# Four transformer layers on one core: closing steps moved between stages, and half 1 of three feed-forward blocks run two chunks behind half 0

## The chip, the core and the metric

The kernel runs on one core of a Trainium2 chip. A core has five engines with instruction streams of their own: TensorE (PE in the profile, its weight loads PEld), VectorE (DVE), ScalarE (ACT), GpSimd (POOL) and SyncE (SP), which issues most of the DMAs. The metric is the device time of one execution in microseconds.

## The reference

Four layers follow each other over 1024 tokens of 256 features, in float32. Each is an attention, a residual add and a LayerNorm without weights, and then a feed-forward block with the same ending. The eight stages differ; cut to what matters here:

```python
def _layernorm(x): return (x - mean(x)) / sqrt(var(x) + 1e-5)
x = _layernorm(x + L0_attn(x))   # windowed differential attention, 16 heads of 128, 4 key heads
x = _layernorm(x + L0_ffn(x))    # 8 experts, the two best per token
x = _layernorm(x + L1_attn(x))   # causal, 16 heads of 128
x = _layernorm(x + L1_ffn(x))    # ternary weights, SiLU gate, RMS norm of the hidden 1024
x = _layernorm(x + L2_attn(x))   # causal, 16 heads of 16
x = _layernorm(x + L2_ffn(x))    # 4-bit weights, tanh GELU gate, hidden 2048
x = _layernorm(x + L3_attn(x))   # causal, 16 heads of 128, normed queries and keys
x = _layernorm(x + L3_ffn(x))    # 64 experts of 64, the eight best, and a shared one

def L3_ffn(h):
    probs = softmax(h @ router_w.T)
    top = top_8(probs); comb = zeros; comb[top] = probs[top] / sum(probs[top])
    out = sum over e of comb[:, e] * (silu(h @ Wg[e].T) * (h @ Wu[e].T)) @ Wd[e].T
    return out + sigmoid(h @ shared_gate.T) * shared(h)

def L0_ffn(h):
    top2 = top_k(h @ Wr, 2); p = softmax(top2.values)
    return sum over the two of p * ((silu(h @ Wg[e]) * (h @ Wu[e])) @ Wd[e])
```

## The kernel before, in words

The tokens are eight tiles of 128 rows, `x[:, t, :]`, kept in on-chip memory; `xT` holds them turned, so that TensorE can contract over the features. Tiles 0 to 3 are half 0, tiles 4 to 7 half 1; two neighbouring tiles are a pair. The stages are the functions `attn0, ffn0, attn1, ffn1, attn2, ffn2, attn3, ffn3`, called in turn by `four_layers` (L2008), each with memory pools of its own. The eight banks of the matmul memory are shared out anew for each stage: wide tiles of two banks each, the rest single banks. All weights go through ten buffers of the pool "w".

Between the stages a LayerNorm is due. `norm_half` (L191) does four tiles: statistics (`add_stats`, L202 and L203), a root by a ScalarE Sqrt (`rsqrt`, L220, and a reciprocal, L221) or by a GpSimd power (`power`, L213 and L214), and the scaling on VectorE (`norm_tile`, L206). `transpose_two` (L163) turns one pair: four transposes (L171) and a copy (L178). By default `four_layers` turns all four pairs at the start of a stage, and it calls `layernorm` after attention two and attention four.

Inside `k.in_order()` the order of the instructions on PE, ACT, DVE and POOL is the program's own. Outside of it, as in the three feed-forward blocks here, the framework's scheduler sets the order by its own estimate, the earlier in the program the sooner, and may put later instructions where it finds an engine free. A tile's memory is reused when its last reader is done.

*Attention one* (`attn0`) runs 32 units (four groups of heads by eight tiles) in a hand-written pipeline: in iteration i the scores and exponentials of unit i (L659, L667), the mix of unit i-1 (L675 to L695), the values and output projection of unit i-3 (L704 to L722, added to x at L233). In the last group its `close` (L558) ends a pair in four steps, one in each iteration: statistics, root, norm with a DMA of the rows to DRAM (L570) and the turning, router product (L159) with the two best experts (L579 to L582).

*Mixture one* (`ffn0`) makes from these indices a table of slots (to L868), gathers token rows (L226), and runs 23 blocks of 128 rows through the experts' weights (L897, L916), which must be in place as one tile.

*Attention two* (`attn1`) first gathers each token's two results (16 indirect DMAs, L226). Its `close` (L1078) adds the results of a pair (L1082), norms it by `rsqrt` and turns it. After each `close` up to six pieces of the first group's queries are projected (`project_next`: L152, and a copy on ACT, L997); the 16 pieces need only the first pair.

*The three feed-forward blocks* `ffn1` (L1192), `ffn2` and `ffn3` (by `ffn`, L288) go over chunks of 128 hidden units (8, 16 and 33 chunks); for each chunk over both halves of the tokens: gate and up products into two banks (L152, in `ffn1` L1208), the hidden values on ACT and DVE, and the down product (L303, L1234) added up in `acc`, two wide tiles with both halves side by side. `add_ffn` (L310) then copies `acc` (L317), turns it back (L321), adds it to x (L233, L327) and calls `norm_half` for each half.

*Attention four* (`attn3`) runs four groups of heads by eight tiles by four heads. `Pipe` (L385) takes one unit (tile, head) at a time: scores (L281), mask, maximum, exponential (L241, L246, L251), reciprocal and scaling on POOL (L258, L259), turned by L268 and copied (L272). Three units after a tile's last head its values (L1869, L1876) and its output projection (L733, added at L233) follow, a step in each unit. *Mixture four* (`ffn3`) starts with the router for all eight tiles (L159 with `wr`, then the shared expert's gate with `ws`), softmax, the eight best (L1931, L1932), the scaling, two splits into three bfloat16 parts (`split3`) and their turning (`transpose_comb`, L340 and L344) into two tiles `combT`; each chunk spreads its rows of `combT` over the hidden units by a product (L947).

Of the kernel before, what the change touches and what calls it, by code (L numbers as in the profile page):

```python
# [42 lines left out]
class Kit:  # L43
# [244 lines left out]
    def ffn(self, chunks, count, hidden, beside=iter(())):  # L288

        nc = self.nc
        acc = [self.wide() for _ in range(NC)]
        for i, (size, gate, up, down, more) in enumerate(chunks):
            for half in range(2):
                g, u = self.bank()[:size], self.bank()[:size]
                self.project(g, gate, half * HALF, HALF)
                self.project(u, up, half * HALF, HALF)
                h = hidden(g, u, half, more)  # L300
                next(beside, None)
                for m in range(NC):
                    nc.tensor.matmul(  # L303
                        acc[m][:, half * HALF : (half + 1) * HALF],
                        lhsT=down[:, m * P : (m + 1) * P], rhs=h,
                        start=i == 0, stop=i == count - 1,
                    )
        return acc

    def add_ffn(self, acc, scale=None):  # L310

        nc = self.nc
        yT = [self.tile("p4", [P, T]) for _ in range(NC)]
        for half in range(2):
            cols = slice(half * HALF, (half + 1) * HALF)
            for m in range(NC):
                (nc.scalar.copy if m else nc.vector.tensor_copy)(yT[m][:, cols], acc[m][:, cols])  # L317
        for t in range(NT):
            ps = self.bank()[:, :D]
            for m in range(NC):  # L320
                nc.tensor.transpose(  # L321
                    ps[:, m * P : (m + 1) * P], yT[m][:, t * P : (t + 1) * P], self.ident
                )
            if scale is None:
                self.add_rows(t, ps)
            else:
                nc.vector.scalar_tensor_tensor(  # L327
                    self.x[:, t, :], ps, scale[:, t : t + 1], self.x[:, t, :],
                    ALU.mult, ALU.add,
                )  # L330
            if t % 4 == 3:
                self.norm_half(t // 4)

    def transpose_comb(self, parts, n):

        combT = self.tile("w", [3 * n, T], BF16)
        for half in range(2):
            ps = self.bank()[: 3 * n]
            for i in range(4):
                self.nc.tensor.transpose(  # L340
                    ps[:, i * P : (i + 1) * P],
                    parts[:, half * 4 + i].rearrange("p s e -> p (s e)"), self.ident,
                )
            self.nc.vector.tensor_copy(combT[:, half * HALF : (half + 1) * HALF], ps)  # L344
        return combT
# [23 lines left out]
class Pipe:  # L369
# [37 lines left out]

    def finish(self):
        while self.first or self.second or self.queued or self.rest:
# [34 lines left out]
def attn0(k, a):  # L444
# [106 lines left out]

    wr = k.tile("const", [P, NC, 8], tag="wr")
    nc.sync.dma_start(out=wr, in_=a["L0_ffn_Wr"].rearrange("(c p) e -> p c e", p=P))
    logits, k.top = (k.tile("const", [P, NT, 8], tag=n) for n in ("logits", "top"))
    k.which = k.tile("const", [P, NT, 8], U32, tag="which")
    k.rows = k.tile("dram", [T, D], tag="moe_rows")

    def close(t, last=False):  # L558


        stats = k.tile("st", [P, 4, 2], tag="stats", bufs=2)
        k.add_stats(t, stats)
        yield
        k.add_stats(t + 1, stats)
        at = t % 4
        rstd = (k.rsqrt if last else k.power)(stats[:, at : at + 2, 1], 2, LN_EPS)
        yield
        for i in range(2):
            k.norm_tile(t + i, stats, rstd[:, i : i + 1])
        nc.sync.dma_start(  # L570
            out=k.rows[t * P : (t + 2) * P, :].rearrange("(t p) d -> p t d", p=P),
            in_=k.x[:, t : t + 2, :],
        )
        k.transpose_two(t)
        yield
        ps = k.bank()[:, :16].rearrange("p (t e) -> p t e", t=2)
        for i in range(2):
            k.project_rows(ps[:, i, :], lambda c: wr[:, c, :], (t + i) * P)
        nc.vector.tensor_copy(logits[:, t : t + 2, :], ps)  # L579
        for i in (t, t + 1):  # L580
            nc.vector.max(k.top[:, i, :], logits[:, i, :])
            nc.vector.max_index(k.which[:, i, :], k.top[:, i, :], logits[:, i, :])  # L582

    runs = [(g, half) for g in range(4) for half in range(2)]
    closing = {}
    with k.in_order():
# [4 lines left out]
        for i in range(len(units) + 3):  # L591
# [27 lines left out]
            for _ in ending:  # L619
                pass  # L620
            for steps in closing.values():
                next(steps, None)
            if i >= 3 and units[i - 3][0] == 3:
                t = units[i - 3][1]
                if t % 2 == 0:
                    closing[t] = close(t, t == NT - 2)
                    next(closing[t])
        for steps in closing.values():
            for _ in steps:
                pass  # L630
# [1466 lines left out]
```

## Time and profile before

| | us |
|---|---|
| median of 3 runs | 2358.47 (2358.36 to 2358.62) |
| the profiled execution, its own time | 2366.98 |
| its span, first to last instruction | 2365.3 |
| attention one, to its last add to x (L233) | 0 to 299.4 |
| mixture one, to its last expert product | to 402.5 |
| attention two, to its last output projection | to 982.1 |
| ternary block, to its last down product | to 1036.9 |
| attention three, to its last add to x | to 1272.7 |
| second block, to its last down product | to 1450.3 |
| attention four, to its last output projection | to 1964.5 |
| mixture four, to its last down product | to 2349.7 |

The mean granted TensorE clock is 0.970 of full speed. All times below are of the profiled execution, counted from its first instruction. In a timeline each line is start, length, engine, line of the kernel, operation, what it writes and reads with shapes, the count, and in brackets the idle time before it with what ended it. In the chain of waits each piece is start, length, engine, tile and line.

### The profile page before, as it was taken

The page shows a single profiled execution, that of the slowest core. Times are in us where ns is not written, and L with a number is a line of the kernel's source. Part 1 is how long each engine was busy: PE and PEld are TensorE (multiplying, and loading weights), DVE is VectorE, ACT ScalarE, POOL GpSimd, SP SyncE. Part 2 cuts the span into 40 slices and gives each one's busy share as a digit, 9 for nine tenths or more (in the row PEclk, how much of TensorE's full clock was granted, in tenths as well). Part 3 has the DMA queues.
Part 4 walks back from the last instruction along what each step waited for, and adds up shares of the span by engine and source line. Part 5 has one row for each costly group of instructions (what it writes and reads, how often), then busy time and mean ns, then how long its engine had stood idle before and what let it go on. Part 6 is the DMA issues. An engine that isn't in the chain of part 4 may idle for free.

```text
span 2365.3 us, 25450 instructions
## 1 busy us (share of the span) xinstructions
PE 2175.3 (92%) x8595; PEld 1228.6 (52%) x8595; DVE 1219.0 (52%) x2726; ACT 904.5 (38%) x2345; POOL 493.5 (21%) x633
## 2 busy tenths in 40 slices
PE   7999767899999999998898998899999997999997
PEld 4666544566656655664444443455555564444443
DVE  5677556465665646555763445544544554222223
ACT  3666523334343434344453222454544451111111
POOL 4333221222232323321110000332222220000000
PEclk9999879899999999989999999999999998999999
DMA  5100163011102101013100010000000000111000
GB/s 167 43 18 20 41 196 109 25 41 36 50 22 63 54 27 41 19 54 119 53 2 10 27 54 27 2 1 18 1 18 10 10 1 18 36 45 45 20 2 18
DMA packets 59250, 92.24 MB, mean 39 GB/s; under 512 B 8976, under 2 KB 33616, under 8 KB 59120
## 3 DMA queue, kind: packets, MB, share of 16 engines
q1 hardware_dynamic: 54208, 78.15, 10.5%
q0 software_dynamic: 4912, 12.46, 1.9%
q8 instruction: 69, 1.13, 0.2%
q14 instruction: 61, 0.50, 0.1%
HBM read 69.76 MB, written 17.17 MB: 37 GB/s over the span
## 4 chain that ended last, share of the span: by engine, by line
PE 78%; DVE 10%; ACT 6%; issue 2%; DMA 2%; POOL 1%; SPq 1%; another core or an unknown queue 0%; ACTq 0%; DVEq 0%; POOLq 0%
PE bank L152 23%; PE wide L281 10%; PE wide L303 7%; PE bank L1063 5%; PE bank L268 5%; PE bank L1869 5%; PE bank L159 4%; PE bank L733 3%; ACT e L667 2%; PE bank L1048 2%; PE bank L1460 1%; PE bank L722 1%; PE bank L1208 1%; PE bank L897 1%; ACT pt L1485 1%
## 5 line engine op out<-in xcount | busy, mean ns | idle before, releaser
L152 PE MATMUL bank<-xT,w 128*128 128x512 f32 (+2 forms) x1520 | 663.3, 566 | 3.3 <-DVE xT L178 2.5
L152 PEld LDWEIGHTS bank<-xT,w 128*128 128x128 f32 (+1 forms) x1520 | 288.5, 195 | 282.2 <-issue 259.3
L259 POOL TENSOR_SCALAR p<-p,st 128x128 f32<-128x128 f32 (+7 forms) x256 | 191.8, 749 | 678.5 <-DVE st L258 535.7
L281 PE MATMUL wide<-k,q 128*128 128x512 f32 (+3 forms) x768 | 290.3, 487 | 3.6 <-ACT p L251 2.7
L272 ACT COPY pt<-bank 128x512 f32<-128x512 f32 (+3 forms) x384 | 171.0, 480 | 307.5 <-PE bank L268 304.3
L281 PEld LDWEIGHTS wide<-k,q 128*128 128x128 f32 x768 | 142.5, 190 | 140.5 <-issue 125.3
L246 DVE TENSOR_REDUCE st<-wide 128x1 f32<-128x128 f32 (+7 forms) x256 | 194.1, 758 | 14.4
L303 PE MATMUL wide<-t,w 128*128 128x512 f32 (+1 forms) x392 | 187.5, 600 | 3.9 <-DVE t L1737 2.4
L268 PE MATMUL bank<-ident,p 128*128 128x128 f32 x1152 | 169.2, 274 | 18.7 <-POOL p L259 18.6
L268 PEld LDWEIGHTS bank<-ident,p 128*128 128x128 f32 x1152 | 137.7, 141 | 83.0 <-issue 38.8
L1987 DVE TENSOR_TENSOR t<-t,bank 128x512 f32<-128x512 f32 (+1 forms) x66 | 45.4, 688 | 258.0 <-PE bank L152 249.5
L1986 ACT ACTIVATE t<-bank 128x512 f32<-128x512 f32 (+1 forms) x66 | 39.4, 597 | 324.4 <-PE bank L152 314.8
L1063 PE MATMUL bank<-pt,v 128*128 128x512 f32 (+3 forms) x384 | 139.3, 487 | 0.0
L241 DVE TENSOR_TENSOR wide<-wide,causal 128x128 f32<-128x128 f32 x256 | 74.7, 292 | 121.7 <-PE wide L281 120.7
L1869 PE MATMUL bank<-pt,v 128*128 128x512 f32 x288 | 137.2, 596 | 0.0
L251 ACT ACTIVATE p<-wide,st,factor 128x128 f32<-128x128 f32 (+7 forms) x128 | 106.5, 832 | 71.2 <-DVE st L248 70.5
L303 PEld LDWEIGHTS wide<-t,w 128*128 128x128 f32 (+1 forms) x392 | 68.0, 189 | 109.4 <-issue 47.4
L251 ACT ACTIVATE p<-wide,st 128x128 f32<-128x128 f32 (+7 forms) x128 | 95.1, 743 | 65.1 <-DVE st L246 64.4
L159 PE MATMUL bank<-w,xT 128*128 128x512 f32 (+2 forms) x288 | 116.0, 540 | 0.5 <-ACT v L541 0.5
L667 ACT ACTIVATE e<-wide,st 128x128 f32<-128x128 f32 x256 | 90.1, 378 | 51.3 <-DVE st L659 36.6
L1485 ACT ACTIVATE pt<-wide 128x1024 f32<-128x1024 f32 (+3 forms) x96 | 75.7, 811 | 70.0 <-PE wide L1479 68.1
L233 DVE TENSOR_TENSOR x<-bank,x 128x256 f32<-128x256 f32 x120 | 49.8, 421 | 88.8 <-PE bank L1048 34.5
(310 smaller groups left out, 3059.5 us busy)
## 6 DMA issues: line engine op xcount, KB each, us to landing
w<-in_L_ffn_gate_up_dram SPq DMA_DIRECT2D x16, 512.0 KB
w<-in_L_attn_Wq_dram SPq DMA_DIRECT2D x12, 512.0 KB
w<-in_L_attn_Wo_dram SPq DMA_DIRECT2D x12, 512.0 KB
rows<-parts SPq DMA_DIRECT2D x16, 256.0 KB
w<-in_L_ffn_down_dram SPq DMA_DIRECT2D x8, 512.0 KB
w<-in_L_attn_Wk_dram SPq DMA_DIRECT2D x7, 512.0 KB
w<-in_L_attn_Wv_dram SPq DMA_DIRECT2D x6, 512.0 KB
moe_results<-y SPq DMA_DIRECT2D x23, 128.0 KB
```

The source lines that it names most:

```text
L152: self.nc.tensor.matmul(out, lhsT=weight(c), rhs=self.xcols(c, lo, n), start=c == 0, stop=c == NC - 1)
L159: self.nc.tensor.matmul(out, lhsT=self.xcols(c, lo, n), rhs=weight(c), start=c == 0, stop=c == NC - 1)
L246: nc.vector.tensor_reduce(top, scores[:, :n], axis=AX.X, op=ALU.max, negate=True)
L251: nc.scalar.activation(probs[:, :n], scores[:, :n], AF.Exp, bias=top, scale=1.0 if scale is None else scale, accum_out=total,)
L259: self.nc.gpsimd.tensor_scalar(probs[:, :n], probs[:, :n], total, 1.0, ALU.mult, ALU.mult)
L268: self.nc.tensor.transpose(ps[:, i * P : (i + 1) * P], probs[:, (lo + i) * P : (lo + i + 1) * P], self.ident,)
L272: self.nc.scalar.copy(pts[lo // 4][:, :n, slot * P : (slot + 1) * P], ps[:, : n * P].rearrange("p (b q) -> p b q", b=n),)
L281: self.nc.tensor.matmul(s[:, lo : lo + m], lhsT=query, rhs=key(lo, m), start=True, stop=True)
L303: nc.tensor.matmul(acc[m][:, half * HALF : (half + 1) * HALF], lhsT=down[:, m * P : (m + 1) * P], rhs=h, start=i == 0, stop=i == count - 1,)
L667: nc.scalar.activation(e[:, r, f, b, :], sc[:, r, f, b, :], AF.Exp, bias=top[:, at : at + 1], accum_out=total[:, at : at + 1],)
L1063: nc.tensor.matmul(out[:, lo:], lhsT=values[g, b][:, h * P : (h + 1) * P], rhs=pts[b // 4][:, b % 4, lo:], start=b == 0, stop=b == 4 * hal ...
L1869: nc.tensor.matmul(out, lhsT=values[i][:, g * P : (g + 1) * P], rhs=pts[i // 4][:, i % 4, :], start=i == 0, stop=i == b,)
```

## The change

1. `attn0` loses its closing steps. `four_layers` calls `layernorm` after it and turns all pairs at the start of `ffn0`; `ffn0` writes the rows to DRAM in two DMAs of one half each and makes the router product, maxima and indices for all tiles at once.
2. In `attn1` the closing of a pair is split in three functions, and query pieces are put between them: with counts 0, 3, 4 and 5 for the four pairs, all but one between the adding and the root, one between the root and the norm.
3. `ffn` and `ffn1` run half 1 two chunks behind half 0 (`LAG`), and end half 0 (copies, turning, adds, norm) before the last three half-chunks of half 1. `add_ffn` takes one half.
4. `attn3` gets a `close` for a pair in eight steps: power, norm, turning, router product with the shared gate in a 65th column, softmax (the gate by an exponential instead of a sigmoid), eight best, combination, and for each of the two groups of experts a split and a turning. One step follows each unit of the last group. What is left runs in `ffn3` after half 0 of the first chunk (`before`). The `layernorm` after `attn3`, the turning at the start of `ffn3` and its router part go.

The core of the diff:

```diff
-    def ffn(self, chunks, count, hidden, beside=iter(())):
+    LAG = 2
+    def ffn(self, chunks, count, hidden, before=iter(())):
         acc = [self.wide() for _ in range(NC)]
+        held = {}
+        def add_up(i, half):
+            size, gate, up, down, more = held[i] if half == 0 else held.pop(i)
+            g, u = self.bank()[:size], self.bank()[:size]
+            self.project(g, gate, half * HALF, HALF)
+            self.project(u, up, half * HALF, HALF)
+            h = hidden(g, u, half, more)
+            for m in range(NC):
+                nc.tensor.matmul(
+                    acc[m][:, half * HALF : (half + 1) * HALF],
+                    lhsT=down[:, m * P : (m + 1) * P], rhs=h, start=i == 0, stop=i == count - 1,
+                )
+        for i in range(count + self.LAG):
+            if i < count:
+                held[i] = next(chunks)
+                add_up(i, 0)
+            for _ in before:
+                pass
+            if i == count - 1:
+                self.add_ffn(acc, 0)
+            if i >= self.LAG:
+                add_up(i - self.LAG, 1)
+        self.add_ffn(acc, 1)
...
-    def transpose_comb(self, parts, n):
+    def transpose_comb(self, parts, combT, t):
+        n = combT.shape[0]
+        ps = self.bank()[:n, : 2 * P]
+        for i in range(2):
+            self.nc.tensor.transpose(
+                ps[:, i * P : (i + 1) * P], parts[:, i].rearrange("p s e -> p (s e)"), self.ident
+            )
+        self.nc.vector.tensor_copy(combT[:, t * P : (t + 2) * P], ps)
...
@@ attn1
-        for t in range(0, NT, 2):
+        for t, count in ((0, 0), (2, 3), (4, 4), (6, 5)):
+            add_results(t)
+            for i in range(count - 1):
+                project_next()
+            take_root(t)
+            if count:
+                project_next()
             close(t)
-            for _ in range(6 if pieces[0][:2] == (make_queries, 0) else 0):
-                if pieces[0][:2] == (make_queries, 0):
-                    project_next()
...
@@ ffn1 (add_up(i, half) is the loop's former body)
+    def finish(half):
+        ps = k.bank()[:, :4]
+        for i in range(4):
+            at = (4 * half + i) * P
+            nc.tensor.matmul(
+                ps[:, i : i + 1], lhsT=squares[:, at : at + P], rhs=k.ones, start=True, stop=True
+            )
+        norm = k.rsqrt(ps, 4, float(np.finfo(np.float32).eps), 1.0 / 1024)
+        k.add_ffn(acc, half, norm)
+    for i in range(8 + k.LAG):
+        if i < 8:
+            add_up(i, 0)
+        if i == 7:
+            finish(0)
+        if i >= k.LAG:
+            add_up(i - k.LAG, 1)
+    finish(1)
...
@@ attn3
+    wr = k.tile("w", [P, NC, 65])
+    k.combT = [k.tile("w", [99, T], BF16) for _ in range(2)]
+    def close(t):
+        at = t % 4
+        rstd = k.power(stats[t // 4][:, at : at + 2, 1], 2, LN_EPS, tag="root")
+        yield
+        for i in range(2):
+            k.norm_tile(t + i, stats[t // 4], rstd[:, i : i + 1])
+        yield
+        k.transpose_two(t)
+        yield
+        ps = k.bank()[:, :130].rearrange("p (t e) -> p t e", t=2)
+        for i in range(2):
+            k.project_rows(ps[:, i, :], lambda c: wr[:, c, :], (t + i) * P)
...
+        nc.scalar.activation(probs, probs, AF.Exp)
+        nc.scalar.activation(gate, ps[:, :, 64], AF.Exp, scale=-1.0)
+        yield
...
+        for group in range(2):
+            yield
+            parts = k.tile("t2", [P, 2, 3, 33])
+            k.split3([parts[:, :, i, :] for i in range(3)], comb[:, :, group, :], [P, 2, 33])
+            k.transpose_comb(parts, k.combT[group], t)
+    def close_on():
+        if k.closing and next(k.closing[0], k) is k:
+            k.closing.pop(0)
...
+        if g == 3:
+            if b % 4 == 0:
+                stats[b // 4] = k.tile("st", [P, 4, 2], tag="stats", bufs=2)
+            k.add_stats(b, stats[b // 4])
+            if b % 2:
+                k.closing.append(close(b - 1))
...
@@ ffn3
-    k.add_ffn(k.ffn(chunks(), 33, hidden))
+    k.ffn(chunks(), 33, hidden, (step for steps in k.closing for step in steps))
@@ four_layers
-            mine = {ffn0: (), attn1: (), ffn1: (), ffn2: (), attn2: (0, 2)}
+            mine = {attn1: (), ffn1: (), ffn2: (), attn2: (0, 2), ffn3: ()}
-            if stage in (attn1, attn3):
+            if stage in (attn0, attn1):
                 k.layernorm()
```

## The prediction

> **What bounds the kernel now.** I read first the page's engine totals, then the busy time by stretches (one row for each stage boundary that the diff touches), then the timeline at those boundaries, and last the chain of waits in the end of the first attention.
>
> ```profile
> PE 2175.3 (92%) x8595; PEld 1228.6 (52%) x8595; DVE 1219.0 (52%) x2726; ACT 904.5 (38%) x2345; POOL 493.5 (21%) x633
> ```
>
> TensorE is busy 92% of the span, so 190 us are left in which it is not. Where they lie is seen by stretches (start:end, length, then busy us of PE, PEld, DVE, ACT and POOL, the granted clock, DMA share):
>
> ```profile
> 278.00:299.00 21.00, 15.47 (x66) 11.38 (x65) 7.37 (x30) 6.13 (x17) 2.85 (x8) 0.84 0.24 74
> 299.00:322.00 23.00, 5.88 (x48) 4.53 (x47) 12.71 (x58) 3.07 (x4) 4.54 (x5) 0.60 0.94 305
> 417.00:448.00 31.00, 22.54 (x81) 17.52 (x80) 13.98 (x37) 11.05 (x19) 6.99 (x8) 0.79 0.12 37
> 1034.00:1049.00 15.00, 9.89 (x45) 8.09 (x45) 12.02 (x38) 4.06 (x7) 1.27 (x1) 0.61 0.27 88
> 1446.00:1464.00 18.00, 9.79 (x37) 5.72 (x38) 13.70 (x42) 3.58 (x6) 0.00 (x0) 0.81 0.25 84
> 1860.00:1951.00 91.00, 89.35 (x360) 54.28 (x358) 50.09 (x145) 49.05 (x107) 24.20 (x35) 1.00 0.03 7
> 1965.00:1991.00 26.00, 13.06 (x97) 12.57 (x98) 17.85 (x59) 4.96 (x6) 0.00 (x0) 0.71 0.14 41
> 1991.00:2347.00 356.00, 355.21 (x855) 151.11 (x853) 91.07 (x132) 39.40 (x66) 8.52 (x29) 1.00 0.08 25
> 2347.00:2366.00 19.00, 4.66 (x20) 2.32 (x20) 11.01 (x37) 2.95 (x5) 0.00 (x0) 0.71 0.16 56
> ```
>
> The bodies are TensorE-bound (355.21 of 356 us in the last mixture, 89.35 of 91 in the fourth attention's last heads); the boundaries are VectorE chains under which TensorE waits. The widest is between attention four and its mixture:
>
> ```profile
> 1962.50 1.99 PE L733 MATMUL bank<-w,ot 128*128 128x256 f32 x8 [0.79 <-DVE ot L1876]
> ...
> 1972.32 0.69 DVE L1923 TENSOR_REDUCE st<-bank 128x8 f32<-128x512 f32 x1 [2.45 <-PE bank L159]
> ...
> 1990.83 4.76 PE L152 MATMUL bank<-xT,w 128*128 128x512 f32 x8
> ```
>
> From the end of the last output projection (1964.49) to the first gate product (1990.83) are 26.3 us. At the end of the second mixture:
>
> ```profile
> 1448.35 1.98 PE L303 MATMUL wide<-t,w 128*128 128x512 f32 x4 [2.39 <-DVE t L1737]
> 1449.51 1.29 DVE L317 COPY p<-wide 128x512 f32<-128x512 f32 x2 [1.22 <-PE wide L303]
> ...
> 1462.08 1.91 PE L159 MATMUL bank<-w,xT 128*128 128x512 f32 x2
> ```
>
> Both halves of the accumulator are copied only after half 1 is done, and attention four starts 11.8 us after the last down product. In the first attention the pairs' closing steps stand in the chain itself:
>
> ```profile
> 261.79 0.54 DVE x L206
> 262.33 0.04 issue
> 262.37 0.88 PE bank L171 x4
> 263.25 0.02 issue
> 263.28 0.69 DVE xT L178
> ```
>
> **What the Trainium skill says.** "TensorE: Matmul & The Clock Gate", Part 1: the matrix clock falls to half after an idle window of about 3.4 us and comes back after as long a busy one. The trace agrees: the granted clock is 0.60 to 0.84 in these stretches and 1.00 in the bodies, and eight L722 took 3.78 us at 282.30 and 1.99 at 290.21. "ScalarE: Activation LUTs", What ACT_TABLE_LOAD costs: 1283 ns and a drain after it. The load is 1.28 us here; no drain shows (the load at 1948.92 is followed by its Sqrt at 1950.21). "Perfetto Trace Analysis", Tensor Engine Instruction: ScalarE and VectorE run strictly in their order. At 429.56 a Sqrt whose input was ready at 421.48 runs behind six query copies.
>
> **The change, part by part**, all against the profiled span.
>
> *Attention four to the last mixture.* Removed: the 26.3 us. Put in their place, by pairs: of TensorE per pair four L171 (two pairs took 1.09, so 0.57), eight router loads and products (28 took 3.24: 0.93; the gate's own 32, 3.68 us, go into the same 65 columns), four turns of weights (16 L340 took 3.71: 0.93), together 2.43. Three pairs lie in the last heads, which have no slack: 7.3, less the 0.8 and 1.45 us for which TensorE waited at 1962 and 1952, of which I take little: +7. Pair four lies in the mixture: +2.4. Per pair VectorE gets some 35 small operations, about 9.5 us at 0.17 to 0.43; eight units of some 3.4 us have 27 us and VectorE is 55% busy there, so this fits, but is queued ahead of the next unit's mask and maximum: I take +1 in all. POOL gets a power of 0.69 in place of the Sqrt and its table. Each step has a unit of its own, so what waits behind it is the next unit's softmax, then L268. Pair four's chain from the last L733 is 16 to 19 us (add 0.43, statistics 0.65, power 0.95, norm 0.75, turn and copy 1.9, router 1.9, softmax with a table load 2.5, top eight 2.5, two splits 3, turns 2). The half 1 that needs it starts after three half-chunks of 5.37 = 16.1 us, and needs the weights some 1.7 later: a stall of 0 to 4, taken as 2. Bank release 0.5. Sum: -26.3 + 7 + 1 + 2.4 + 2 + 0.5 = **-13.4** (-20 to -5). SP now issues the router's two loads at attention four's start instead of at 1498, and three of the ten weight buffers (router, two turned weights) are taken before the mixture; its first weights were issued from 1635 on, so neither is a bound.
>
> *Ends of three blocks.* Half 0 ends three half-chunks ahead, so its copies, turns, adds and norm lie beside TensorE's bodies. Instructions in the bodies stay; a bank tile more or less isn't asked for. Last block: after its L317 at 2348.91 only four tiles follow. VectorE then has four adds (1.42), four statistics (2.25) from 2350.83: 2354.5; root and reciprocal 0.6; norm 1.4: 2356.5 instead of 2360.33. The output DMA was issued at 2360.36 and moves with it: **-3.9**. Second mixture block: copies end 1450.9, first add frees a bank at 1451.8, turn 0.6 and copy 0.7 of the already normed half, attention four's rows start at 1453.6; before, they started at 1462.08, stopped, and went on at 1464.26, worth 1463.2: -9.6, less 1 for half 0's work on the last chunks: **-8.5** (-10 to -5). Ternary block: 1036.93 to 1048.96 were 12.0. Squares now 1037.35 to 1038.3, root and reciprocal 0.55, first scaled adds 1039.3 to 1040.6, turn, copy, first product 1042.3: -6.6. Against it its ScalarE is busy 1.84 of 2.91 us per half-chunk and gets a root between Silus, two loads of 1.28; VectorE gets 6.5 us in 8.7 where 4.2 are taken: +1.6. **-5** (-7 to -1).
>
> *Second attention's start.* Roots no longer wait behind six copies. Pair 2: statistics 421.48, root 422.9 behind two copies, turn done 424.9 (before 431.75). Pair 4: statistics 428.9, root 430, turn done 431.8 (441.8). Pair 6: 435.9, 436.4, 437.9 (447.6). Then four queries of 0.86 are still due before keys: 441.4 against 447.44: **-6** (-8 to -2). The gathers (the last issued at 425.18) bound it from below.
>
> *First attention undone.* Score exponentials of its last units end 7.15 us apart where nothing is put between and 7.8, 9.6, 7.35, 7.14 after 246.18: without closings the last end is 274.8, not 278.08. Then three turns of 5.1 with the first at 4.9: the last add ends at 290.3, not 299.40. Then in series what was spread: statistics, root, reciprocal 1.2, four norms 1.4, last turn and copy 1.6, routers (32, of which 16 lie under the norm) to 7.2, one copy and eight maximum and index pairs of 0.36, 3.1: 10.3 to the last index, where one pair took 7.5. Then 9.4 to the first gather as now: 310.0 against 316.25. Half 0's norm falls in the drain and may hold a copy there: +1. SP: the rows' two writes stand ahead of the expert weights; these start when the last L710 frees their place, 288 against 296.24, and took 20 us, so they land by 311 even with 2 us of stall, before the first expert product at 316. **-5** (-8 to +3; the upper end if the roots fall between exponentials or the weights wait for the second write).
>
> Sum: -13.4 - 3.9 - 8.5 - 5 - 6 - 5 = -41.8. The profile's own time is 2366.98 (span 2365.3), 8.5 over the median 2358.47; a difference carries over: 2358.5 - 41.8 = 2316.7, 2317.
>
> **Rivals.** One: closings cost in attention four what they cost in attention one, 3.3 us for four units, 0.83 a step; 24 steps are 20 us in place of the 1: 2336. For it: the same in-order queues. Against: here each step has a unit and TensorE, not a chain through ScalarE, is the bound. Chance 0.14. Two: the copies of half 0 still wait for half 1 (L317 did so while VectorE idled from 2341.98), as both lie in one tile: the block ends keep their tails, +17.4: 2334. Against: in the new order the copies stand ahead of half 1's last three. Chance 0.08. Three: the first attention gives back 3 instead of gaining 5, 2325; it shares the forecast's case. Slower: the closing steps' waits stand wholly in the unit chain, at the 2.5 us that turn, copy and statistics took at 261.79 to 264.5; 24 steps are 60 us in place of the 1: 2376. It decides above (41.8 + 1) / 24 = 1.8 us a step. Chance 0.05. No change, if the rivals add up: 0.02. Forecast 0.71.
>
> **Range.** The bounds of the parts added in squares give some 9 either way; the first two rivals reach to 2336. 2302 to 2338. A difference of 0.2% (4.7 us) is what a measurement of this kernel tells from none. Faster 0.93, same 0.02, slower 0.05.
>
> **What would show it.** Right: the first gate product within 3 us of the last L733, and L317 in two groups some 15 us apart; first gather near 310; turns at 424, 431, 437. Wrong: TensorE waiting for VectorE between L281 and L268 in attention four; gaps in the first three half-chunks; expert products waiting for weights.

## The result, and the profile after

The changed kernel takes 2347.44 us (median of 5 runs, 2345.31 to 2349.54) where the kernel before took 2358.62 beside it: a ratio of 0.9955 (0.9944 to 0.9966), a gain of 11.2 us where 41.8 were forecast. The span of its profiled execution is 2347.5 us.

A second profiled execution of the kernel before (first experiment) has a span of 2358.7, so it, not the first one of 2365.3, is the one to subtract from. The stages, measured from TensorE's products:

| stretch | before, first | before, second | after | forecast of the difference |
|---|---|---|---|---|
| start to the first expert product | 322.2 | 321.3 | 321.9 | -5 |
| mixture one's last product to attention two's first score | 47.6 | 41.8 | 37.8 | -6 |
| ternary block, first to last down product | 43.8 | 43.8 | 51.7 | +1.6 |
| from there to attention three's first wide product | 17.9 | 16.3 | 13.2 | -6.6 |
| second block, first to last down product | 163.8 | 163.8 | 165.0 | +1 |
| from there to attention four's first row product | 11.8 | 11.7 | 7.8 | -9.6 |
| attention four, first product of values to last output projection | 455.3 | 455.5 | 467.6 | +8 |
| from there to the last block's last down product | 385.2 | 386.6 | 369.7 | -21.4 |
| from there to the end | 15.5 | 15.7 | 10.7 | -3.9 |

Against the second execution the rows give +0.6, -4.0, +7.9, -3.1, +1.2, -3.9, +12.1, -16.9 and -5.0. They sum to -11.1; the stages that the table leaves out differ by some us either way and cancel.

The engine totals of the page:

```profile
PE 2168.4 (92%) x8563; PEld 1222.0 (52%) x8563; DVE 1228.8 (52%) x2799; ACT 913.7 (39%) x2358; POOL 492.8 (21%) x637
```

TensorE's share has not risen. Busy time of the changed kernel by stretches, with the columns as before:

```profile
294.00:322.00 28.00, 11.20 (x75) 9.85 (x72) 15.01 (x74) 3.07 (x4) 4.86 (x5) 0.56 0.86 276
...
1850.00:1941.00 91.00, 83.27 (x346) 50.83 (x345) 61.29 (x205) 42.64 (x99) 21.42 (x32) 1.00 0.02 7
...
1973.00:2337.00 364.00, 357.30 (x865) 152.50 (x864) 101.11 (x180) 44.08 (x73) 8.44 (x29) 0.99 0.09 27
```

Attention four's last heads were full (89.35 of 91 us) and now leave TensorE idle for 7.7 of 91: the closing steps brought waits and not only work. The last block, 355.21 of 356 before, now has 6.7 us of idle time. The boundary itself went as forecast (timeline of the changed kernel):

```profile
1965.10 1.99 PE L701 MATMUL bank<-w,ot 128*128 128x256 f32 x8 [1.11 <-DVE ot L1944]
1966.93 3.60 PE L152 MATMUL bank<-xT,w 128*128 128x512 f32 x8
...
1972.06 1.08 PE L159 MATMUL bank<-w,xT 128*128 128x65 f32 x8 [0.87 <-DVE xT L178]
...
1978.37 0.76 PE L351 MATMUL bank<-ident,t 128*99 128x128 f32 x4 [3.46 <-DVE t L363]
```

The first gate product follows the last output projection at once. But the turning of pair four's splits (L351) then stands in TensorE's queue for 3.46 us until VectorE has made the splits.

### The profile page after: what moved, and what is told of

The parts are those of the page before. It is cut to its first block, busy times and chain, and to the rows that moved or that the text cites. A ratio compares the mean times of both kernels' runs of the same rounds, so it can differ in the third digit from the quotient of the medians.

```text
span 2347.5 us, 25446 instructions
## 1 busy us (share of the span) xinstructions
PE 2168.4 (92%) x8563; PEld 1222.0 (52%) x8563; DVE 1228.8 (52%) x2799; ACT 913.7 (39%) x2358; POOL 492.8 (21%) x637
## 4 chain that ended last, share of the span: by engine, by line
PE 68%; issue 11%; DVE 10%; ACT 6%; DMA 2%; POOL 1%; SPq 1%; DVEq 0%; ACTq 0%; POOLq 0%
PE bank L152 18%; PE wide L281 9%; PE bank L1047 5%; PE wide L306 5%; PE bank L268 5%; PE bank L1937 4%; PE bank L159 3%; ACT e L635 3%; PE bank L701 3%; PE bank L1032 2%; PE bank L1464 1%; PE bank L881 1%; PE bank L1202 1%; DVE st L627 1%; PE bank L690 1%
## 5 line engine op out<-in xcount | busy, mean ns | idle before, releaser
L281 PE MATMUL wide<-k,q 128*128 128x512 f32 (+3 forms) x768 | 290.6, 487 | 3.7 <-ACT p L251 2.8
L281 PEld LDWEIGHTS wide<-k,q 128*128 128x128 f32 x768 | 142.1, 190 | 136.6 <-issue 121.3
L306 PE MATMUL wide<-t,w 128*128 128x512 f32 (+1 forms) x392 | 188.5, 603 | 4.9 <-DVE t L2026 3.2
L268 PE MATMUL bank<-ident,p 128*128 128x128 f32 x1152 | 169.3, 274 | 21.4 <-POOL p L259 20.0
L268 PEld LDWEIGHTS bank<-ident,p 128*128 128x128 f32 x1152 | 137.7, 141 | 85.6 <-issue 39.0
L306 PEld LDWEIGHTS wide<-t,w 128*128 128x128 f32 (+1 forms) x392 | 68.3, 189 | 109.4 <-issue 48.0
L159 PE MATMUL bank<-w,xT 128*128 128x512 f32 (+3 forms) x320 | 122.8, 521 | 1.7 <-DVE xT L178 0.9
```

Source lines behind the costliest of these rows:

```text
L159: self.nc.tensor.matmul(out, lhsT=self.xcols(c, lo, n), rhs=weight(c), start=c == 0, stop=c == NC - 1)
L268: self.nc.tensor.transpose(ps[:, i * P : (i + 1) * P], probs[:, (lo + i) * P : (lo + i + 1) * P], self.ident,)
L281: self.nc.tensor.matmul(s[:, lo : lo + m], lhsT=query, rhs=key(lo, m), start=True, stop=True)
L306: nc.tensor.matmul(acc[m][:, half * HALF : (half + 1) * HALF], lhsT=down[:, m * P : (m + 1) * P], rhs=h, start=i == 0, stop=i == count - 1,)
```

## The experiments

Unless said otherwise each kernel is the changed kernel with one edit. The kernel before, run beside each, took 2358 us in some sessions and 2365 to 2366 in others (those of *later*, *roots on GpSimd*, *rows first*, *steps apart*, *left out* and attention one's second run), of which some 6 us lie in attention two's start (38 and 44 us from mixture one's last product to the first score, with the same code). So the ratios to the kernel before of the same session are compared, and stages that an edit leaves alone serve as a measure of chance. In the profiles with an untouched ternary block its body took 51.1 to 52.2 us, the last block's (first to last down product) 361.3 to 365.1; smaller differences there say nothing.

**The kernel before, again.** No edit.

> The kernel before, unchanged, for a second profiled execution. The first one took 8.5 us more than the median of the others. Theory: these 8.5 us lie where its TensorE ran at a clock of 0.79, in the query products of attention two (24 L152 in 7.72 us at 418.38), so here attention two's first score product (L281) starts near 443 and not at 450.1, and the span is near 2357. Rival: the 8.5 us are spread over all stages, or lie elsewhere, and L281 starts at 450 again.

Its profiled execution has a span of 2358.7 (ratio 1.0004, 0.9996 to 1.0012). Busy time at attention two's start:

```profile
405.00:444.00 39.00, 22.25 (x87) 16.67 (x88) 19.32 (x52) 13.58 (x22) 15.54 (x16) 0.78 0.20 58
```

L281 starts at 443.37. Of the 6.6 us by which the first span is longer 5.8 lie in that stretch; 2.9 in attention three and smaller differences of both signs make up the rest. So over a third of the 17.8 us that the two first spans show is no gain. The clock is low in this execution too (0.78 in the first row), so my reason, the clock, is not the whole of it.

**Attention one's exchange undone.** `attn0` and `ffn0` as before, twice:

```diff
+            for steps in closing.values():
+                next(steps, None)
...
-    for t in range(NT):
-        k.project_rows(ps[:, t, :], lambda c: wr[:, c, :], t * P)
```

> The changed kernel with attention one's closing steps and mixture one's router as in the kernel before. Theory from the two traces: the exchange is worth nothing, because the 5.4 us by which attention one ends earlier are used up by the router in series, so the first expert product stays within 1 us of 321.9 and the median is 2347 to 2348. Rival, the prediction's step: the change gained 5 there, so this is 2352.

> The changed kernel with attention one and mixture one as before, a second time: are its 4.7 us the exchange or a chance of the clock? If the exchange: the first expert product at 318 to 319.5, where the changed kernel has 321 to 325, and a ratio to before under 0.9945. If chance: 321 to 322, 0.9955 to 0.9965.

Ratios 0.9933 (0.9920 to 0.9946) and 0.9951 (0.9935 to 0.9967); the changed kernel has 0.9955 and, a second time, 0.9966 (0.9952 to 0.9979). The first expert product comes at 318.1 and 319.1, in eleven profiles with the exchange at 321.0 to 325.0. So my first expectation, no effect, was wrong: beside these kernels the exchange costs some 3 us. The second ratio lies between what I had said for an effect and for chance. One reason is seen in the changed kernel's timeline of TensorE:

```profile
297.14 2.89 PE L159 MATMUL bank<-w,xT 128*128 128x8 f32 x14
...
299.88 0.88 PE L171 MATMUL bank<-ident,x 128*128 128x128 f32 x3
300.55 3.85 PE L159 MATMUL bank<-w,xT 128*128 128x8 f32 x18
```

Three of the last pair's four turns (L171 at 299.88) stand behind fourteen router products of other tiles (L159), and the 32 router products take 0.21 us each in a stretch where the clock is 0.56. In the prediction 16 of them lay under the norm; here the first starts at 297.14, when the norm (L206, to 297.24) is just done. What stays open: the same instructions of attention one took 321.3 and 322.2 in the kernel before. Half clock was granted there for 37.5 us between 240 and 330, and for 27.3 in the two kernels here; why, no run shows.

**Attention four's closing steps undone.** `attn3` and the router as before:

```diff
-                    close_on()
...
+    for t in range(NT):
+        k.project_rows(logits[:, t, :], lambda c: wr[:, c, :], t * P)
```

> The changed kernel with attention four without closing steps and the last mixture's router as in the kernel before, in series. Theory from the two traces: the closing steps cost attention four 12.3 us and the mixture some 6 in stalls and added products, against the 26.3 us gap and the 0.6 that go; undoing loses only 3 to 8: 2350 to 2355. Attention four, from its first row product to its last output projection, is 12 us shorter than in the changed kernel. Rival, the prediction's step: 13.4 us, so 2361.

2355.46 us, 0.9985 (0.9976 to 0.9994): 0.0030 more than the changed kernel, about 7 us. Attention four's stretch is 455.3 again, the mixture's 388.9. The steps are worth 7, not 13.4.

**Half 0 ended last.** `add_ffn(acc, 0)` and `finish(0)` after the loop:

```diff
-            if i == count - 1:
-                self.add_ffn(acc, 0)
...
+        self.add_ffn(acc, 0)
         self.add_ffn(acc, 1)
```

> The changed kernel, half 1 still two chunks behind, but half 0's copies, turning, adds and norm come after the last half-chunk of half 1 in all three blocks. Theory: what half 0's early end gains after the last product it costs before it, so the ternary block ends 3 us earlier than in the changed kernel (its last half-chunks lose their 8 us of stall), the second block 3 later, the last 2 later: 2347 to 2351. Rival, the prediction's steps: early ends were worth 17.4 us, so 2365.

0.9951 (0.9940 to 0.9963), the same as with early ends. The ternary block's body is 43.8 (51.7) and what follows 16.0 (13.2): the early end loses 5.2 there. Second block: 163.9 and 11.7 (165.0 and 7.8): it gains 2.8. Last block: 358.8 and 15.0 (363.8 and 10.7): it gains nothing, 0.7 the other way. Three early ends that were forecast at 17.4 us lose 3 in the stages and gain nothing clear of chance in the ratio, and the question is what they cost inside the bodies. The last 17 us before the ternary block's last down product, in the kernel before (second execution) and the changed kernel:

```profile
1015.00:1032.00 17.00, 16.41 (x70) 11.73 (x68) 7.87 (x12) 9.07 (x18) 7.45 (x6) 1.00 0.20 61
```

```profile
1018.00:1035.00 17.00, 13.67 (x52) 9.21 (x52) 10.64 (x26) 11.23 (x16) 3.68 (x4) 0.90 0.20 63
```

TensorE was busy for 16.41 us at full clock, and now is for 13.67 at 0.90. The timeline of the changed kernel's ternary block:

```profile
1016.36 1.53 PE L1227 MATMUL wide<-t,w 128*128 128x512 f32 x4 [0.94 <-ACT t L183]
...
1017.69 0.69 DVE L330 COPY p<-wide 128x512 f32<-128x512 f32 x1 [0.59 <-PE wide L1227]
...
1018.32 1.05 PE L1237 MATMUL bank<-ones,p 128*128 128x1 f32 x8 [0.43 <-POOL p L1224]
...
1020.95 7.37 PE L1202 MATMUL bank<-parts,w 128*128 128x512 f32 x24 [0.37 <-DVE x L340]
...
1026.86 2.37 DVE L206 TENSOR_SCALAR x<-x,st,st 128x256 f32<-128x256 f32 x4
...
1029.15 0.68 DVE L184 TENSOR_TENSOR t<-t,t 128x512 fp32r<-128x512 f32 x1
...
1029.88 0.74 PE L1227 MATMUL wide<-t,w 128*128 128x512 f32 x2 [1.09 <-DVE t L184]
1031.13 1.53 PE L1227 MATMUL wide<-t,w 128*128 128x512 f32 x4 [0.51 <-ACT t L183]
1033.52 1.53 PE L1227 MATMUL wide<-t,w 128*128 128x512 f32 x4 [0.86 <-ACT t L183]
```

Half 0's last products (L1227), the sums of squares (L1237) and the turns (left out here) stand in TensorE's order ahead of half 1's gate products, with waits of 0.94, 0.43 and 0.37 us. Then TensorE does the gate and up products of all three half-chunks that are left in one go (24 L1202). Only down products are left behind them, and these wait 1.09, 0.51 and 0.86 us for half 1's hidden values, with nothing to fill the time. The first of the three waits for L184, which ran behind the scaling of half 0's norm (L206). The next five kernels take suspects away.

**Later.** The end one half-chunk later:

```diff
             if i >= self.LAG:
                 add_up(i - self.LAG, 1)
+            if i == count - 1:
+                self.add_ffn(acc, 0)
```

> The changed kernel, half 0's end (copies, turning, adds, norm) one half-chunk of half 1 later in all three blocks. Theory: in the changed kernel TensorE stands in front of half 0's turns (waits of 0.9, 0.4 and 0.4 us in the ternary block, 0.8 and 1.8 in the others); a half-chunk put ahead covers these. The ternary block, from its first to its last down product, falls from 51.7 to 49 to 50 us, the second block's from 165.0 to 164, the last one's from 363.8 to about 361.5; what follows the last products stays; median near 2342. Rival, ScalarE's roots and table loads hold back the hidden values: no change in the ternary block, 2346.

0.9963 (0.9951 to 0.9975); the ternary block takes 52.3, the second 167.7, the last 362.3. In the ternary block the waits at half 0's end shrink from 1.74 to 1.32 us in all, but at the end of the block TensorE waits 1.35 and 1.96 us for the last hidden values, behind which nothing is left to do. In the second block a wait of 2.39 us for hidden values stands ahead of half 0's turns. My expectation was wrong in two blocks of three; the last one's 1.6 lie within chance.

**Roots on GpSimd.** Half 0's roots by `power`:

```diff
-        norm = k.rsqrt(ps, 4, float(np.finfo(np.float32).eps), 1.0 / 1024)
+        norm = (k.rsqrt if half else k.power)(ps, 4, float(np.finfo(np.float32).eps), 1.0 / 1024)
```

> The changed kernel with half 0's roots (the ternary block's own and the three norms') as a power on GpSimd, so that ScalarE loads no table between half 1's last hidden values. Rival (ScalarE): of the ternary block's 7.9 lost us the 3.1 go for which TensorE waited at L1227 after 1028, so 51.7 becomes 48.5; 2344. Theory (TensorE's order alone): 51 to 52, 2347.

0.9956 (0.9942 to 0.9969), the ternary block 52.4. Its timeline:

```profile
1032.46 2.34 DVE L206 TENSOR_SCALAR x<-x,st,st 128x256 f32<-128x256 f32 x4 [1.13 <-POOL st L214]
...
1034.72 0.68 DVE L184 TENSOR_TENSOR t<-t,t 128x512 fp32r<-128x512 f32 x1
```

ScalarE is free, but the scaling now waits for GpSimd in VectorE's queue, and half 1's low part (L184), on which TensorE waits, stands behind it. The wait changed engines.

**The norm called later, and left out.** The first calls half 0's norm after the loop; the second leaves out the norm of half 0's four tiles after this block; the third in addition takes the block's own root to GpSimd:

```diff
-        self.norm_half(half)
+        if norm:
+            self.norm_half(half)
```

> The changed kernel; in the ternary block half 0's copies, turning and adds stay where they are, its norm comes after the last half-chunk. Theory now: it is the norm, by its statistics and scaling on VectorE (4.3 us) as much as by its root on ScalarE, that holds back half 1's last hidden values, so that moving the root to GpSimd gained nothing; without it the block falls from 51.7 to 48 to 48.5 (2.4 us of moved TensorE work and 1.7 of waits remain) and what follows grows by 1 or 2. Rival, TensorE's wait at half 0's turns, which stays here: 51 to 52.

> The changed kernel with half 0's LayerNorm after the ternary block left out (its copies, turns and adds stay), so that it can't be put back among half 1's hidden values, as the scheduler did with the norm that was called later. If the norm holds them back (ScalarE 1.6 us of table and root between two Silus, VectorE 4.3 us): first to last down product 51.5 falls to 48 to 49.5. If TensorE's order (waits of 1.7 us at half 0's turns and 2.4 us of moved products) and the block's own root are the cause: 50.5 to 52.

> As the one before, and the ternary block's own root for half 0 as a power on GpSimd, so that ScalarE loads no table for half 0. If norm and table loads are what holds the hidden values back: 47 to 48.5, that is 43.8 plus 2.4 us of moved products plus 1.7 of waits. If TensorE's order alone: 51 again.

The first has 0.9962 (0.9948 to 0.9975) and 51.5 us, but tests nothing: the scheduler put the norm back among half 1's hidden values (L206 at 1030.56, where the block's last down products are at 1037.2), as it may outside `in_order`. With the norm left out the block takes 49.9 us (ratio 0.9938, 0.9925 to 0.9951), with the root moved too 50.9 (0.9952, 0.9936 to 0.9969). My theory of the norm had said 48 to 49.5 and 47 to 48.5, its rival 50.5 to 52 and 51: the block gained 1 to 2 us, less than the theory said. What is left is seen in the stretches of the kernel without the norm (TensorE's busy time first, its clock third from the end):

```profile
1022.00:1026.00 4.00, 3.06 (x12) 1.52 (x10) 2.15 (x4) 2.79 (x5) 1.35 (x2) 1.00 0.02 8
1026.00:1030.00 4.00, 3.52 (x16) 3.03 (x16) 1.23 (x4) 2.13 (x3) 1.21 (x1) 0.67 0.00 0
1030.00:1034.00 4.00, 4.00 (x13) 3.31 (x12) 1.39 (x4) 1.33 (x2) 0.00 (x0) 0.50 0.02 4
```

After the waits at half 0's end the granted clock falls to half, and half 1's products run behind it at half speed. So the body must be divided into waits and clock. From its first to its last down product, in us:

| kernel | body | TensorE idle in it | half clock granted in it |
|---|---|---|---|
| before, second execution | 43.8 | 0.5 | 0 |
| changed | 51.7 | 4.4 | 3.41 |
| changed, second profile | 51.2 | 4.0 | 3.41 |
| later | 52.3 | 4.7 | 7.72 |
| roots on GpSimd | 52.4 | 4.3 | 7.54 |
| norm called later | 51.5 | 4.6 | 3.41 |
| norm left out | 49.9 | 2.3 | 6.83 |
| norm left out, root on GpSimd | 50.9 | 3.0 | 6.83 |
| half 0 ended last | 43.8 | 0.9 | 0 |

The idle time is the body less TensorE's busy time. Two of the rows that it is taken from, the changed kernel and the one without the norm:

```profile
983.40:1035.05 51.65, 47.20 (x189) 33.62 (x187) 27.61 (x50) 30.03 (x50) 18.72 (x15) 0.97 0.16 52
```

```profile
992.40:1042.30 49.90, 47.55 (x189) 35.26 (x187) 23.33 (x37) 27.21 (x47) 18.77 (x15) 0.93 0.17 53
```

In the seven profiles whose ternary block is that of the changed kernel the idle time is 3.9 to 4.5 us, and half clock 3.41, in one of them 4.91. So the norm does hold TensorE up: without it 1 to 2 us of the waits go. But half clock was granted for 6.83 us in these two kernels, 3.41 more than in the changed one. As the clock is halved, that is worth at most 1.7 us, an estimate from the granted clock, and about as much as the shorter waits brought. In the changed kernel's second profile the body of 51.2 us divides so, against the kernel before: 3.5 us more idle time, 1.2 for the eight turns, and 2.8 by which the busy time of the same 180 other products is longer (46.04 us, not 43.29). Half clock explains at most 1.7 of these 2.8; for the rest no run shows a cause.

**Rows first.** Attention four turns half 1 just before its rows:

```diff
+    pieces += [(k.transpose_two, t) for t in (4, 6)]
     pieces += [(make_rows, t) for t in range(4, 8)] + [(norm_rows, 1)]
```

> The changed kernel, attention four turns only half 0 at its start and half 1's pairs just before their rows. Theory: the first row product waited at 1453.03 behind half 1's turns in TensorE's queue; now it stands 5.4 us after the last down product and not 7.8, and the first product of values (L1937) is earlier by as much, 51.9 and not 54.3 after it: 2345. Rival, VectorE's norm of half 1 is what the rows wait for, in its queue: the values stay at 54, 2347.

0.9942 (0.9928 to 0.9955). The changed kernel's timeline at this place, and then this one's:

```profile
1451.15 2.08 PE L171 MATMUL bank<-ident,x 128*128 128x128 f32 x8 [2.67 <-DVE x L206]
...
1453.03 14.57 PE L159 MATMUL bank<-w,xT 128*128 128x512 f32 x32
```

```profile
1450.98 1.09 PE L171 MATMUL bank<-ident,x 128*128 128x128 f32 x8 [0.85 <-DVE x L233]
...
1453.54 2.84 PE L159 MATMUL bank<-w,xT 128*128 128x512 f32 x6 [1.47 <-DVE xT L178]
```

In the changed kernel all sixteen turns stand ahead of the first row product, and the last eight wait 2.67 us for half 1's norm. Here the rows start 4.75 us after the last down product (7.8), and attention four ends 518.4 us after it instead of 521.9. The first product of values came at 44.6 and not at the 51.9 that I expected, but attention four takes 6 us longer from there on, so that time is no measure of the gain.

**Steps apart.** Each turning of a split a unit after its split; pair four's steps over two half-chunks:

```diff
-            k.transpose_comb(parts, k.combT[group], t)
+            k.turns.append((parts, k.combT[group], t))
...
-            for _ in before:
+            for _ in zip(range(99 if i else 6), before):
```

> The changed kernel, each turning of a split (L351) a unit after its split, and in the last mixture pair four's first six steps after half 0 of chunk 0, the others after half 0 of chunk 1. Theory: TensorE stood 3.5 us in attention four and 3.5 in the mixture before turns whose split was issued in the same step. Attention four, from its first product of values to its last output projection, falls from 467.6 to 464, the mixture's end after it from 369.7 to 366.5; 2340. Rival, the closing steps' VectorE work delays the units and the wait only moves: 467 and 369, 2347.

0.9927 (0.9913 to 0.9941). Attention four's stretch is 463.7, where ten profiles without the edit show 466.7 to 467.7; the mixture's, 368.3, lies within chance. There TensorE still stands for 1.95 us before a down product (L306 at 1983.41), where it stood for 3.46 before the turn. The waits in attention four, in the changed kernel:

```profile
1891.54 0.77 PE L268 MATMUL bank<-ident,p 128*128 128x128 f32 x5 [1.37 <-POOL t L1820]
...
1895.62 0.43 PE L351 MATMUL bank<-ident,t 128*99 128x128 f32 x2 [1.60 <-DVE t L363]
```

The second is the kind that goes: five such, 3.46 us, of which the last turn keeps one of 1.67 (at 1965.58). The first stays, and the view names a fill of two columns (L1820) as its end. But the scaling of the unit ran ahead of that fill, and the other engines' timeline shows what held it back:

```profile
1887.67 0.19 ACT L251 ACTIVATION_READ_ACCUMULATOR p<-wide,st,factor 128x1 f32 x1
...
1890.24 0.21 DVE L1807 MATCH_REPLACE8 t<-st,t 128x64 f32<-128x64 f32 x1
1890.36 0.15 DVE L258 RECIPROCAL st<-st 128x1 f32<-128x1 f32 x1
...
1890.69 0.80 POOL L259 TENSOR_SCALAR p<-p,st 128x640 f32<-128x640 f32 x1 [4.83 <-DVE st L258]
1891.42 0.10 POOL L1820 MEMSET t<- 128x2 f32 x1
```

The row's sum was there at 1887.86, but its reciprocal (L258) ran 2.5 us later, since VectorE was busy with the last tile's add and statistics and with a closing step (L1801 to L1807). TensorE waits before L268 three times in the last heads, 0.55, 0.90 and 1.37 us. At the other two the statistics of a tile stood ahead of the reciprocal, and once a closing step's power (L214 at 1877.02) ahead of the scaling. The kernel before has no such wait in its last heads, and they are the same with the steps apart.

**The changed kernel again, and the best of both.** No edit; and attention one and mixture one as before, the ternary block's half 0 ended last, rows first, steps apart, the last block's half 0 later with its root on GpSimd.

> The changed kernel, unchanged, beside the two below on one chip. Attention one to the first expert product 322 to 324 us; ternary block 51.7 from its first to its last down product and 13 from there to attention three's first wide product; attention two's start 38 or 44 us after mixture one's last product, as this chip has it (the two chips before differed by 6 us there). Ratio to before 0.9955.

> Attention one and mixture one as in the kernel before; ternary block's half 0 ended after the last half-chunk; attention four turning half 1 just before its rows; turns a unit after their splits; last block's half 0 ended one half-chunk later, its root on GpSimd; the rest as in the changed kernel. Added up from the runs: -4.7 -5.2 -3.4 -5.3 -2.5 = -21 against the changed kernel, a ratio to before of 0.9865. If the first attention's gain of 4.7 was a chance of the clock: 0.9885. Attention one to the first expert product 318 to 321.

0.9966 (0.9952 to 0.9979) and 0.9900 (0.9885 to 0.9916), on one chip. The second is faster than both kernels, 2333.43 us beside 2358.33. It gains 16 us over the changed kernel and not 21: the last block did not gain its 2.5, the ternary block and what follows gained 3.4 and not 5.2, and the first expert product comes at 319.1, 1.9 and not 4.7 earlier than beside it.

## Why the prediction was wrong

- *Attention four to the last mixture*, forecast -13.4: -7 (attention four's steps undone; -9.8 by the table, if the last block's 5.0 below is left out of it). The gap went, and the 7 us of TensorE's work came as forecast (in the last heads L171 takes 1.8, L159 3.0 and L351 2.6 us). The term "+1 in all" for VectorE's queue was mis-sized: attention four grew by 5 us beyond that work. TensorE stands for 3.5 us in front of turns whose split was issued in the same step, and for 2.8 in front of units whose reciprocal stood behind closing steps in VectorE's queue; about 1 us of other waits went. The second kind I had named and put too low, the first, the closing step's own TensorE instructions, I had not looked for. "A stall of 0 to 4, taken as 2" was 3.5 and 0.9.
- *Ends of three blocks*, -3.9, -8.5 and -5: with before's second execution 0, -2.7 and +4.8. The step that failed is "so its copies, turns, adds and norm lie beside TensorE's bodies. Instructions in the bodies stay". The tails did shrink. But half 0's turns are TensorE's own work and stand in its order with their waits, its root and norm stand ahead of half 1's hidden values on ScalarE and VectorE, and half clock followed. The price of the early end in the bodies, put at 1.6 in the ternary block, 1 in the second and nothing in the last, was 7.9, 1.2 and 5.0. It is the largest miss, 11.5 us. Taking only half 0's end out of the bodies shows the price; how it divides between these causes is shown in part. The tails fell short too, by 8.1 us in all. In the second block "attention four's rows start at 1453.6", 3.3 us after the last product, overlooked that half 1's turns stand ahead of them (7.8; rows first). In the ternary block the tail shrank by 3.1 and not 6.6, and half of that difference is the one between the kernel before's two executions. A slip of the sum was small beside this: 6.5 us of VectorE's time on top of 4.2 in 8.7 are 2.0 too many, not 1.6.
- *Second attention's start*, -6: -4.0, right in kind. The turns started at 422.0, 427.9 and 433.7, where 424.9, 431.8 and 437.9 were said for their ends. The other 5.8 us of the two first traces' difference belong to that execution of the kernel before, not to the change.
- *First attention undone*, -5 (-8 to +3): +0.6, and +3 against the undone kernels. The last add came at 294.0 and not 290.3: a table load and a root (1.6 us from 276.57 on) and half clock (eight L690 in 3.49 us at 279.85, 1.99 in the next unit) fell in the drain, for which the prediction had put 1 us; the chain to the last index took 12.5 and not 10.3.
- Of the rivals, the second (half 0's copies wait for half 1) is refuted: L330 copies half 0 at 1017.69, ahead of half 1's last products. The first put the closing steps' cost too high (20 us, where the 12.1 measured hold TensorE's work too), the slower one higher still. The third, the first attention gives back 3, is what the undone kernels show. None named the cost of an early half on TensorE's own queue. The misses had one sign and added up, for which the range left too little room: the parts' own bounds, added in squares, give about 13 us upwards and 8 downwards, not 9 either way, and its upper end came from the rivals.

What stays open: about 1 us of the ternary block's 8, which neither idle time nor the turns nor half clock explain, and how far each wait brought on the half clock. Three edits that moved one engine's share left the block at 51.5 to 52.4 us, and leaving the norm out gained 1 to 2; only taking half 0's end out of the body brought 43.8.

## What to carry to other kernels

Work that moves out of a tail and into a body that is full on TensorE is not free because another engine does most of it: list the moved part's own TensorE instructions and what each waits for, and what its work on the other engines delays that TensorE needs. A turn put a unit behind the split that feeds it took most of the waits away in attention four; in the mixture some of the wait came back before another product, and in the ternary block a later place for half 0's end only moved the waits. Products that need only one half should stand ahead of the other half's turns. And take a second profile of the kernel before: 6.6 us of the first one's span were not there in the second.

## What the runs showed of the hardware

In all profiles half clock is granted for whole multiples of 3.41 us, but for the last such time, which the end cuts off. "TensorE: Matmul & The Clock Gate", Part 1 of the Trainium skill, says that the window is free-running and of that length, and the traces agree; it says that the clock falls after an idle window, and here a partly idle one was enough: in the changed kernel 13 of 15 falls follow 3.41 us in which TensorE was busy for 0.02 to 0.59 of the time, only one of them under 0.1, and two follow 0.77 and 0.80. Windows down to 0.48 kept the full clock. In the ternary block a window with 0.8 us of idle time (the one with 0.77) was followed by 3.41 us of half clock, which is worth up to 1.7 us by the estimate above. So a stall of a microsecond in the middle of a body can cost more than itself, and the same program differs by some three such windows between executions (half clock for 145.4 us in one profile of the kernel before and for 133.0 in the other, 113.5 and 122.6 in the two of the changed kernel).
